# Two transformer layers on one core: x passed through DRAM, the scan's sum made by accumulating transfers, decay and state in shared buffers

## The chip, the cores and the metric

The kernel runs on one core of a Trainium2 chip. The time is device time in microseconds (us), the median of three runs. The five engines have queues of their own: PE (matrix products), DVE and POOL (elementwise work), ACT (activation functions), and SP, which here only issues transfers between DRAM and the on-chip memory. The on-chip memories are SBUF, and PSUM, in which PE's results arrive. One engine's instructions run in the order in which the program lists them; between engines, semaphores order them.

## What is computed

Eight batches of x, each 512 tokens by 256 features in float32, go through two layers with modulated layernorms. Shortened:

```python
# layer 0
h = layernorm(x) * (1 + ca) + sa
x = x + ga * gated_attention(h)            # q^T k over tokens, softmax, v * sum(attn) * gate
h = layernorm(x) * (1 + cb) + sb
x = x + gb * (shared_mlp(h) + top2_of_8_experts(h))
# layer 1, the mixer
h = layernorm(x) * (1 + ca) + sa
raw, gate = split(h @ W_in)
s  = silu(causal_conv(raw) + conv_b)       # 4 taps, 512 channels
ts, Bmat, C = split(s @ W_x)               # 64, 16 and 16 columns
dt = softplus(ts @ W_dt + b_dt)
for t in tokens:                           # state: 512 channels x 16
    state = exp(dt[t] * A) * state + dt[t] * Bmat[t] * s[t]
    y[t]  = sum_over_16(state * C[t])
x = x + ga * (((y + s * D) * silu(gate)) @ W_out)
# layer 1, the feed-forward: weights are -1, 0 or 1, with a scale per output
h = layernorm(x) * (1 + cb) + sb
x = x + gb * w3(gelu(h2(gelu(h1(silu(w1(h)) * w2(h))))))
```

ga and gb have at least 0.25 in magnitude. Each layer has its own sa, ca, ga, sb, cb, gb, one row per batch.

## The kernel before

**A plan.** No loop of the kernel issues instructions directly. The stages record operations with `op(engine, us, fn, r=, w=, need=, lead=, lat=)` (L100): a price in us, what is read and written, and a due time, which `run` (L1061) gives from the stage's start and the share of the stage that is done, less `lead`. `Plan.order` (L135) then simulates the five engines with these prices, takes on each free engine the ready operation that is due first (ACT adds LOOK to those that need another function table), and `emit` writes the instructions in the order of their planned starts. The order on each engine is thus fixed before the run; the times are not. An operation due later than the oldest unplaced one by more than AHEAD is held back (L203).

**Buffers.** A buffer that belongs to a pool (L249) takes a slot when its first operation is placed and gives it back after its last. The pools that matter here: `mm` with 5 PSUM banks for products, `v` with one, `st` with 2 slots of [128, 2, 512], `two` with 5, `xn` with 2, `big` with 8 (feed-forward activations), `hs`, `dt` and `y` with one each. x itself has three fixed slots (L1066); batch b uses slot b mod 3 from its load to the feed-forward.

**Stages.** For each batch (L1096 to L1104): `front` (the attention), `experts`, `mixer`, `ffn`, begun at b x TURN plus 0, FRONT, MIX_AT and FFN_AT. Since MIX_AT and FFN_AT come later than one and two turns, the front and experts of a batch stand beside the mixer of the one before and the ffn of the one before that. A first plan (L1073) holds the setup, the front of batch 0 and `test`, which rounds the 22 blocks of the feed-forward's weights (L1045) and compares them with the originals (L1046). If all are equal, the branch with split float32r activations runs, as it does with these inputs; the other branch is in the program and not run.

**The ends of layer 0.** The experts add their outputs in `acc` (L746, DVE), then POOL multiplies by gb (L751) and adds to x (L753).

**The mixer.** A layernorm of x into xn_m (L763), a transpose into hTm (L764), products ps_raw and the convolution into `hs`, ps_x, a small store of B and C to DRAM (`bc_d`), and dt by two halves of two channel chunks each, with `ab` and `lost` in `st` slots (L800). `y` begins as s times D (L828), hs becomes s times dt (L831). Then come 32 steps u, for 16 states d and two halves h (L844). The rows of B and C come back broadcast to all 128 partitions as brow and crow (L850), and ACT copies brow to PSUM as bp. ACT makes the decays, two exps of 511 columns, in one of three fixed buffers whose column 0 of each chunk is zero (L841). DVE multiplies v = hs x bp (L858) and scans the two chunks as one row of 1024 columns into `st` (L861); the zero restarts the second chunk. POOL multiplies st by crow (L864) and adds it to its half of y (L866). After the last step the gate products ps_g (L873), the product with y, and pa_m (L881); `add_gated` (L476) multiplies pa_m by ga on DVE and adds it to x on POOL.

**The ffn.** A layernorm of x into xn_g (L897), and x stored in `x_d` in DRAM (L898), from where it returns in two loads as `xo` at the end (L1012), is added to the transposed output and stored. Its activations (a_h_sh and a_h_sl are the high and low parts) go to float32r products, ps_h_s and pa_f (L988, L1002). All matrix products are recorded with line L343.

**Loads.** `load` (L313) records a DMA on SP with a lead of 12 us and a latency of 2.0; SP's queue is one list for weights, rows, x and stores. Weights are loaded anew for every batch.

Of the kernel before, what the change touches and what calls it, by code (L numbers as in the profile page):

```python
# [10 lines left out]
ALU = mybir.AluOpType  # L11
# [34 lines left out]
TURN, FRONT, EXPERTS = 235.0, 64.0, 124.5  # L46
MIX_AT, MIX = 221.7, 270.0
FFN_AT, FFN = 531.0, 249.5
FROM, UNTIL = 0.12, 0.949
LOOK = 16.226  # L50
DECAYS, BURST = 3, 1
EARLY, RUSH, SLOW, AHEAD = 19.951, 14.0, 4.404, 69.662
# [14 lines left out]
class Op:  # L67
    __slots__ = ("eng", "us", "fn", "due", "bufs", "succ", "npred", "avail", "lock", "table",
                 "start", "end", "lat", "n", "placed")


class Plan:
# [27 lines left out]
    def op(self, eng, us, fn, r=(), w=(), need=(), lock=False, table=None, lead=0.0, lat=0.0):  # L100
        o = Op()
        o.eng, o.us, o.fn, o.due, o.lock, o.table, o.lat = eng, us, fn, self.due - lead, lock, table, lat
        o.n, o.succ, o.npred, o.avail, o.placed = len(self.ops), [], 0, 0.0, False
# [31 lines left out]
    def order(self):  # L135
# [9 lines left out]
        t, left = 0.0, len(self.ops)  # L145

        def placeable(o):
            want, lines = {}, {}
            for b in o.bufs:
                if b.pool and b.slot is None:  # L150
                    want[b.pool] = want.get(b.pool, 0) + 1
                    if self.pools[b.pool][1]:
                        lines.setdefault(b.line, []).append(b)
# [6 lines left out]
        def place(o):  # L160
# [14 lines left out]
            if e == "SP":  # L175
                free[e] = t + 0.06
                dma = max(dma, t) + us
                o.end = dma + o.lat
            else:
                free[e] = o.end  # L180
                o.end += o.lat
# [10 lines left out]
            for s in o.succ:  # L192
                s.npred -= 1
                s.avail = max(s.avail, o.end + (0.0 if s.eng == e and e != "SP" else self.HOP))
# [4 lines left out]
        while left:  # L199
            placed = False  # L200
            while first < len(by_due) and by_due[first].placed:
                first += 1
            limit = by_due[first].due + self.ahead if first < len(by_due) else 0.0  # L203
# [25 lines left out]
            assert later, "nothing can be placed"  # L229
            t = min(later)  # L230
# [13 lines left out]
def block_kernel(ctx: ExitStack, tc: tile.TileContext, t: dict, out: bass.AP):  # L244
# [8 lines left out]
        "dt": (1, True), "y": (1, True), "sp": (1, True), "st": (2, True), "bcb": (1, True),  # L253
# [42 lines left out]

    for i in range(DECAYS):
        G.memset(fixed([P, 2, S], f"decay{i}").t, 0.0)

    def record(part):  # L300
# [5 lines left out]
        decay = [fixed([P, 2, S], f"decay{i}") for i in range(DECAYS)]  # L306
# [6 lines left out]
        def load(dst, kb, fn, r=(), part=None, lead=12.0, need=()):  # L313
            op("SP", kb * 0.0052, fn, r=r, w=[(dst, part)] if part is not None else [dst], lead=lead,
# [264 lines left out]
        def front(b, x):  # L579
# [76 lines left out]
            for m in range(CH):  # L656
# [5 lines left out]
                    pg.t, [(whgv()[:, k, ms], nT.t[:, k, :]) for k in range(KD)]), r=[whg, nT])  # L662
# [25 lines left out]
        def experts(b, x):  # L688
# [9 lines left out]
            for m in range(CH):  # L698
# [5 lines left out]
                    pv.t, [(w3v()[:, k, ms], hT.t[:, k, :]) for k in range(KD)]), r=[w3, hT])  # L704
# [48 lines left out]
            op("POOL", 2.4, lambda: G.tensor_tensor(x.t, x.t, acc.t, ALU.add), r=[acc], w=[x], lead=RUSH)  # L753


        def mixer(b, x):
# [6 lines left out]
            layernorm(x, xn, f"m{b}", RUSH)  # L763
# [72 lines left out]
            def exps(u):  # L836
                for v in range(u, u + BURST):
                    d, h = v // 2, v % 2
                    for i in range(2):
                        c = 2 * h + i  # L840
                        A.activation(decay[v % len(decay)].t[:, i, 1:], dt.t[:, c, 1:], AF.Exp,  # L841
                                     scale=neg_a.t[:, c, d : d + 1])

            for u in range(2 * DST):  # L844
                d, h = u // 2, u % 2
                da, cs = decay[u % len(decay)], slice(2 * h, 2 * h + 2)
# [7 lines left out]
                if u % BURST == 0:  # L854
                    op("ACT", 1.42 * BURST, lambda u=u: exps(u), r=[dt, neg_a],
                       w=[decay[v % len(decay)] for v in range(u, u + BURST)], table="exp", lead=SLOW)
# [3 lines left out]
                st = buf("st", [P, 2, S], f"st_{b}_{d}_{h}")  # L860
                op("DVE", 2.28, lambda v=v, st=st, da=da: V.tensor_tensor_scan(  # L861
                    st.t.rearrange("p c t -> p (c t)"), da.t.rearrange("p c t -> p (c t)"),
                    v.t.rearrange("p c t -> p (c t)"), 0.0, ALU.mult, ALU.add), r=[da, v], w=[st])
                op("POOL", 2.4, lambda st=st, cc=cc: G.tensor_tensor(  # L864
                    st.t, st.t, over_tokens(cc.t, 2), ALU.mult), r=[cc], w=[st])
                op("POOL", 2.4, lambda st=st, cs=cs: G.tensor_tensor(  # L866
                    y.t[:, cs, :], y.t[:, cs, :], st.t, ALU.add), r=[st], w=[(y, pair(h))])
# [12 lines left out]
            for j in range(NT // 2):  # L880
# [3 lines left out]
                add_gated(x, j, ps, ga, lambda: ga.t, f"tmpm_{b}_{j}")  # L884


        def ffn(b, x):
# [4 lines left out]
            half = 0.5 if fast else 1.0  # L892
# [4 lines left out]
            layernorm(x, xn, f"g{b}", RUSH)  # L897
            op("SP", 2.7, lambda: SP.dma_start(out=x_d[b].t, in_=x.t), r=[x], w=[x_d[b]], lat=2.0)  # L898
# [49 lines left out]
            for g in range(CF // 2):  # L948
                gs = slice(2 * g * P, (2 * g + 2) * P)
                w, (w1, w2) = weights(f"w_f{b}_{g}", [f1[:, :, gs], f2[:, :, gs]], g)  # L950
                for i in range(2):
# [6 lines left out]
                        pv.t, by(lambda k: w2()[:, k, ms], hT, KD)), r=[w] + every, share=half)  # L958
# [50 lines left out]
            for j in range(NT // 2):  # L1009
                ps, xo = mm(f"ps_o{b}_{j}"), buf("two", [P, 2, D], f"xo_{b}_{j}", line="xo")  # L1010
                js = slice(2 * j, 2 * j + 2)
                load(xo, 256, lambda xo=xo, js=js: SP.dma_start(out=xo.t, in_=x_d[b].t[:, js, :]), r=[x_d[b]], lead=RUSH)  # L1012
# [53 lines left out]
        slots_x = [fixed([P, NT, D], f"x_{i}") for i in range(3)]  # L1066
        xs = [slots_x[b % 3] for b in range(B)]
# [28 lines left out]
        for b in range(B):  # L1096
# [6 lines left out]
            run(mixer(b, xs[b]), b * TURN + MIX_AT, MIX)  # L1103
# [65 lines left out]
```

## Time and profile before

| | |
|---|---|
| median of 3 runs | 2246.09 us (2244.88 to 2247.49) |
| the profiled execution | 2246.68 us, its span 2244.9 us |
| mean granted clock of PE | 0.94 |
| moved over the span | 294.52 MB, mean 131 GB/s |

The profile is one execution. Where the stages of some batches stood, first to last start, in us from the start of the span:

| batch | qk | last product of experts (end) | ps_raw, first | first v to last v | pa_m | ps_o |
|---|---|---|---|---|---|---|
| 0 | 58.2 | 206.8 | 220.6 | 279.8 to 442.3 | 475.0 to 483.8 | 760.3 |
| 1 | 237.8 | 403.2 | 434.9 | 502.2 to 672.5 | 716.8 to 723.9 | 1013.7 |
| 2 | 461.4 | 654.0 | 678.0 | 743.2 to 913.0 | 959.0 to 972.9 | 1257.5 |
| 5 | 1206.3 | 1392.9 | 1413.9 | 1479.0 to 1655.5 | 1688.3 to 1702.3 | 1948.2 |
| 7 | 1691.8 | 1878.4 | 1899.5 | 1954.5 to 2102.8 | 2119.3 to 2126.4 | 2236.0 |

In rows of the profile, a group is a line, an engine and an operation with what it writes and reads; busy time and mean of one stand before the second bar's idle time, which is that of the engine just before such instructions, with what released it. A transfer's row has its size and the median from issue to landing.

### The profile page before, as it was taken

Reading aid. Unit: us, or ns where it says so; the run is one execution under the profiler, and the core shown is the slowest. Engines: PE = TensorE matmul, PEld = TensorE weight load, DVE = VectorE, ACT = ScalarE, POOL = GpSimd, SP = SyncE. Lnnn points to the kernel's source line nnn. Section 1 sums busy time; section 2 is a strip of 40 time slices with the busy share of each in tenths; the row PEclk is TensorE's granted clock in tenths of the full one; section 3 lists DMA queues with packets and bytes.
Section 4 is the critical chain, followed back from the end, with each engine's and each line's share of the span. In section 5 each row is a group of like instructions: output and inputs, shape, how many; then the busy total and the mean of one; then the engine's idle time right before and its main releaser. Section 6 shows DMA issues by size and latency. Waiting matters only on the chain.

```text
span 2244.9 us, 22011 instructions
## 1 busy us (share of the span) xinstructions
PE 1973.9 (88%) x6916; PEld 1292.8 (58%) x6916; DVE 1635.1 (73%) x2074; ACT 1691.8 (75%) x2433; POOL 1535.7 (68%) x765
## 2 busy tenths in 40 slices
PE   1897879498999899999999999999999999768587
PEld 0455336245775567656765577656765677445465
DVE  4532589869885898669895998679876988598531
ACT  3522768569987898788988898789988898779442
POOL 1201488969896788567895789678876789399700
PEclk6998889699999999999999999999999999979888
DMA  9226335223453345334443345334533443335333
GB/s 264 77 93 191 88 108 167 79 91 122 142 175 106 112 133 171 112 111 139 158 157 117 115 150 174 116 118 140 170 121 117 140 150 116 120 108 169 103 104 105
DMA packets 186608, 294.52 MB, mean 131 GB/s; under 512 B 14232, under 2 KB 109728, under 8 KB 186480
## 3 DMA queue, kind: packets, MB, share of 16 engines
q1 hardware_dynamic: 186480, 293.01, 41.3%
q8 instruction: 57, 0.93, 0.2%
q14 instruction: 71, 0.58, 0.1%
HBM read 283.94 MB, written 20.55 MB: 136 GB/s over the span
## 4 chain that ended last, share of the span: by engine, by line
PE 67%; POOL 10%; ACT 9%; DVE 9%; issue 3%; DMA 1%; SPq 0%; DVEq 0%; POOLq 0%; ACTq 0%
PE ps_h_s L343 17%; PE pa_e L343 9%; PE ps_e L343 9%; PE ps_sim L343 4%; POOL st L864 4%; POOL y L866 4%; PE pg L343 4%; DVE st L861 3%; PE pv L343 3%; PE pa_m L343 3%; PE ps_qk L343 2%; PE pa_f L343 2%; PE ps_g L343 2%; PE pa_o L343 2%; PE pa_s L343 2%
## 5 line engine op out<-in xcount | busy, mean ns | idle before, releaser
L864 POOL TENSOR_TENSOR st<-st,crow 128x1024 f32<-128x1024 f32 x256 | 608.5, 2377 | 167.4 <-DVE st L861 103.0
L866 POOL TENSOR_TENSOR y<-y,st 128x1024 f32<-128x1024 f32 x256 | 607.7, 2374 | 18.1
L861 DVE TENSOR_TENSOR_SCAN st<-decay,v 128x1024 f32<-128x1024 f32 x256 | 584.6, 2284 | 35.7 <-POOL y L866 17.4
L841 ACT ACTIVATE decay<-dt,neg_a 128x511 f32<-128x511 f32 x512 | 335.8, 713 | 46.5 <-DVE st L861 41.3
L858 DVE TENSOR_TENSOR v<-hs,bp 128x1024 f32<-128x1024 f32 x256 | 313.3, 1224 | 13.6 <-ACT bp L853 8.6
L343 PE MATMUL ps_h_s<-a_h_sh,w_f_h 128*128 128x512 f32 x512 | 212.0, 414 | 35.3 <-DVE a_h_sl L915 31.7
L343 PE MATMUL ps_h_s<-a1h,w_f_h 128*128 128x512 f32 x512 | 220.5, 431 | 16.0 <-DVE a1l L973 14.7
L343 PE MATMUL pa_e<-w_e,ge 128*128 128x256 f32 x1024 | 232.1, 379 | 1.4 <-ACT ge L735 1.4
L343 PE MATMUL ps_e<-hT,w_e 128*128 128x512 f32 x512 | 231.4, 592 | 0.0
L343 PEld LDWEIGHTS pa_e<-w_e,ge 128*128 128x128 f32 x1024 | 194.4, 190 | 44.6 <-issue 15.3
L343 PE MATMUL ps_h_s<-a_h_sl,w_f_h 128*128 128x512 f32 x512 | 204.8, 400 | 0.0
L343 PE MATMUL ps_h_s<-a1l,w_f_h 128*128 128x512 f32 x512 | 202.8, 396 | 0.0
L841 ACT ACT_TABLE_LOAD x146 | 187.3, 1283 | 4.0 <-DVE st L861 1.3
L746 DVE SCALAR_TENSOR_TENSOR acc<-pa_e,rt,acc 128x256 f32<-128x256 f32 x256 | 112.0, 477 | 87.3 <-PE pa_e L343 86.3
L991 ACT ACTIVATE a_h_sh<-ps_h_s,cols 128x512 fp32r<-128x512 f32 x128 | 88.0, 688 | 110.4 <-PE ps_h_s L343 109.4
L915 DVE TENSOR_TENSOR a_h_sl<-ps_h_s,a_h_sh 128x512 fp32r<-128x512 f32 x128 | 87.4, 683 | 96.1 <-ACT ps_h_s L991 95.6
L343 PEld LDWEIGHTS ps_e<-hT,w_e 128*128 128x128 f32 x512 | 97.2, 190 | 92.4 <-issue 79.4
L343 PEld LDWEIGHTS ps_h_s<-a_h_sh,w_f_h 128*128 128x128 f32 x512 | 99.0, 193 | 70.4 <-DVE a_h_sl L915 35.7
L343 PEld LDWEIGHTS ps_h_s<-a1h,w_f_h 128*128 128x128 f32 x512 | 97.9, 191 | 48.9 <-DVE a1l L973 15.5
L735 ACT ACTIVATE ge<-ps_e 128x512 f32<-128x512 f32 x128 | 73.8, 598 | 54.1 <-PE ps_e L343 53.5
L343 PEld LDWEIGHTS ps_h_s<-a1l,w_f_h 128*128 128x128 f32 x512 | 97.9, 191 | 28.0 <-issue 8.7
L343 PE MATMUL ps_sim<-k,q 128*128 128x512 f32 x256 | 113.8, 603 | 0.0
(212 smaller groups left out, 3821.4 us busy)
## 6 DMA issues: line engine op xcount, KB each, us to landing
w_f_h<-fw_d SPq DMA_DIRECT2D x128, 512.0 KB, 3.5
w_e<-in_ew SPq DMA_DIRECT2D x128, 256.0 KB, 3.0
brow<-bc_d SPq DMA_DIRECT2D x128, 256.0 KB, 3.7
crow<-bc_d SPq DMA_DIRECT2D x128, 256.0 KB, 3.9
w_f<-fw_d SPq DMA_DIRECT2D x48, 512.0 KB, 4.0
w_s<-in_sw SPq DMA_DIRECT2D x24, 512.0 KB, 5.6
test<-in_f_h SPq DMA_DIRECT2D x16, 512.0 KB, 7.3
fw_d<-in_f_h SPq DMA_DIRECT2D x16, 512.0 KB, 6.4
```

The costliest lines, as they stand in the source:

```text
L343: T.matmul(ps, lhsT=lhsT, rhs=rhs, start=(i == 0), stop=(i == last))
L735: op("ACT", 0.63, lambda ps=ps, g=ge[m]: A.activation(g.t, ps.t, AF.Gelu), r=[ps], w=[ge[m]], table="gelu", lead=RUSH)
L746: op("DVE", 0.48, lambda ps=ps, n=n, i=i, e=e: V.scalar_tensor_tensor(acc.t[:, n, :], ps.t[:, i * D : (i + 1) * D], comb(n, e), acc.t[:, n ...
L841: A.activation(decay[v % len(decay)].t[:, i, 1:], dt.t[:, c, 1:], AF.Exp, scale=neg_a.t[:, c, d : d + 1])
L858: op("DVE", 1.22, lambda v=v, cs=cs, bp=bp: V.tensor_tensor(v.t, hs.t[:, cs, :], over_tokens(bp.t, 2), ALU.mult), r=[hs, bp], w=[v])
L861: op("DVE", 2.28, lambda v=v, st=st, da=da: V.tensor_tensor_scan(st.t.rearrange("p c t -> p (c t)"), da.t.rearrange("p c t -> p (c t)"), v ...
L864: op("POOL", 2.4, lambda st=st, cc=cc: G.tensor_tensor(st.t, st.t, over_tokens(cc.t, 2), ALU.mult), r=[cc], w=[st])
L866: op("POOL", 2.4, lambda st=st, cs=cs: G.tensor_tensor(y.t[:, cs, :], y.t[:, cs, :], st.t, ALU.add), r=[st], w=[(y, pair(h))])
L915: op("DVE", 0.69, lambda: V.tensor_tensor(lo.t[:, at, :], ps.t, hi.t[:, at, :].bitcast(F32), ALU.subtract), r=[ps, (hi, at)], w=[(lo, at)] ...
L991: put(ps, nxt, m, lambda o, ps=ps, m=m, s=s: A.activation(o, ps.t, AF.Gelu, scale=col(s)[:, m : m + 1]), 0.69, [cols], table="gelu")
```

## The change

It has four parts, and new planner times.

- **x passes through DRAM.** The experts end with acc x gb + x in `acc`, which is stored in `x_d`. The mixer loads it for its layernorm, which works in place in xn; its tail loads x again in two halves (`xm`), adds the gated output in `tmp` and stores the halves in `x_d`. The ffn loads that, normalizes in place, and loads xo as before, now only once fT[0] stands. x has two fixed slots instead of three. `add_gated` is no longer called by the mixer.
- **y is summed by transfers.** The add of POOL (before: L866) becomes a DMA that POOL issues and that adds st to y in SBUF. It is ordered behind the multiply of its step and behind the last accumulate on the same half of y.
- **Decay and state share buffers.** The pool `st` has six slots instead of two; the exps, now of 512 columns, are written in the step's own st slot, and two scans of 512 columns work in place there. The three decay buffers and their clearing go.
- **Orders and planner.** Some products also need the buffers that their followers write (`need=`). The planner learns `move`, a DMA issued from POOL; loads are priced at 0.0032 us a KB instead of 0.0052; if nothing can be placed, the limit of AHEAD is lifted once (`stuck`). Mixer and ffn have turns of their own (TURN_M, TURN_F).

```diff
-TURN, FRONT, EXPERTS = 235.0, 64.0, 124.5
-MIX_AT, MIX = 221.7, 270.0
-FFN_AT, FFN = 531.0, 249.5
-FROM, UNTIL = 0.12, 0.949
-LOOK = 16.226
-DECAYS, BURST = 3, 1
-EARLY, RUSH, SLOW, AHEAD = 19.951, 14.0, 4.404, 69.662
+TURN, FRONT, EXPERTS = 210.53, 82.297, 147.593
+TURN_M, MIX_AT, MIX = 212.288, 264.782, 239.578
+TURN_F, FFN_AT, FFN = 215.967, 519.656, 225.321
+FROM, UNTIL = 0.193, 0.955
+LOOK = 40.478
+EARLY, RUSH, SLOW, AHEAD = 37.621, 10.554, -11.873, 136.563
...
-        "dt": (1, True), "y": (1, True), "sp": (1, True), "st": (2, True), "bcb": (1, True),
+        "dt": (1, True), "y": (1, True), "sp": (1, True), "st": (6, True), "bcb": (1, True),
...
-    for i in range(DECAYS):
-        G.memset(fixed([P, 2, S], f"decay{i}").t, 0.0)
...
-            op("POOL", 2.4, lambda: G.tensor_tensor(x.t, x.t, acc.t, ALU.add), r=[acc], w=[x], lead=RUSH)
+            op("POOL", 2.4, lambda: G.tensor_tensor(acc.t, acc.t, x.t, ALU.add), r=[x], w=[acc], lead=RUSH)
+            op("SP", 1.7, lambda: SP.dma_start(out=x_d[b].t, in_=acc.t), r=[acc], w=[(x_d[b], (0, 1))], lat=2.0,
+               lead=RUSH)
...
-            layernorm(x, xn, f"m{b}", RUSH)
+            load(xn, 512, lambda: SP.dma_start(out=xn.t, in_=x_d[b].t), r=[(x_d[b], (0, 1))])
+            layernorm(xn, xn, f"m{b}", RUSH)
...
+            def exps(u, st):
+                d, h = u // 2, u % 2
+                for i in range(2):
+                    c = 2 * h + i
+                    A.activation(st.t[:, i, :], dt.t[:, c, :], AF.Exp, scale=neg_a.t[:, c, d : d + 1])
+
+            def scans(v, st):
+
+                for i in range(2):
+                    V.tensor_tensor_scan(st.t[:, i, :], st.t[:, i, :], v.t[:, i, :], 0.0, ALU.mult, ALU.add)
...
-                st = buf("st", [P, 2, S], f"st_{b}_{d}_{h}")
-                op("DVE", 2.28, lambda v=v, st=st, da=da: V.tensor_tensor_scan(
-                    st.t.rearrange("p c t -> p (c t)"), da.t.rearrange("p c t -> p (c t)"),
-                    v.t.rearrange("p c t -> p (c t)"), 0.0, ALU.mult, ALU.add), r=[da, v], w=[st])
+                op("DVE", 2.35, lambda v=v, st=st: scans(v, st), r=[v], w=[st])
...
-                op("POOL", 2.4, lambda st=st, cs=cs: G.tensor_tensor(
-                    y.t[:, cs, :], y.t[:, cs, :], st.t, ALU.add), r=[st], w=[(y, pair(h))])
+                op("POOL", 0.88, lambda st=st, cs=cs: G.dma_start(
+                    out=y.t[:, cs, :], in_=st.t, accum_op=ALU.add), r=[st], w=[(y, pair(h))], move=2.8, lat=3.0)
...
-                add_gated(x, j, ps, ga, lambda: ga.t, f"tmpm_{b}_{j}")
+                tmp, xo = buf("two", [P, 2, D], f"tmpm_{b}_{j}", line="tmp"), buf("two", [P, 2, D], f"xm_{b}_{j}", line="xm")
+                js = slice(2 * j, 2 * j + 2)
+                load(xo, 256, lambda xo=xo, js=js: SP.dma_start(out=xo.t, in_=x_d[b].t[:, js, :]),
+                     r=[(x_d[b], j), (y, 0)], lead=RUSH, need=[tmp])
+                op("DVE", 0.69, lambda ps=ps, tmp=tmp: V.tensor_tensor(
+                    tmp.t, ps.t.rearrange("p (i d) -> p i d", i=2), over_tokens(ga.t, 2), ALU.mult),
+                    r=[ps, ga], w=[tmp], lead=RUSH)
+                op("POOL", 1.3, lambda tmp=tmp, xo=xo: G.tensor_tensor(tmp.t, tmp.t, xo.t, ALU.add),
+                   r=[xo], w=[tmp], lead=RUSH)
+                op("SP", 1.4, lambda tmp=tmp, js=js: SP.dma_start(out=x_d[b].t[:, js, :], in_=tmp.t),
+                   r=[tmp], w=[(x_d[b], j)], lat=2.0)
...
-            layernorm(x, xn, f"g{b}", RUSH)
-            op("SP", 2.7, lambda: SP.dma_start(out=x_d[b].t, in_=x.t), r=[x], w=[x_d[b]], lat=2.0)
+            load(xn, 512, lambda: SP.dma_start(out=xn.t, in_=x_d[b].t), r=[(x_d[b], (0, 1))])
+            layernorm(xn, xn, f"g{b}", RUSH)
...
+                     r=[(x_d[b], j), fT[0]], lead=RUSH)
...
-        slots_x = [fixed([P, NT, D], f"x_{i}") for i in range(3)]
-        xs = [slots_x[b % 3] for b in range(B)]
+        slots_x = [fixed([P, NT, D], f"x_{i}") for i in range(2)]
+        xs = [slots_x[b % 2] for b in range(B)]
...
-            run(mixer(b, xs[b]), b * TURN + MIX_AT, MIX)
-            run(ffn(b, xs[b]), b * TURN + FFN_AT, FFN)
+            run(mixer(b), b * TURN_M + MIX_AT, MIX)
+            run(ffn(b), b * TURN_F + FFN_AT, FFN)
```

## The prediction

> **What bounds it now.** I read the busy shares and the slices first, then single stretches, then what ends the waits. Columns of the slices: one digit per 56 us.
>
> ```profile
> PE 1973.9 (88%) x6916; PEld 1292.8 (58%) x6916; DVE 1635.1 (73%) x2074; ACT 1691.8 (75%) x2433; POOL 1535.7 (68%) x765
> ...
> PE   1897879498999899999999999999999999768587
> ...
> POOL 1201488969896788567895789678876789399700
> PEclk6998889699999999999999999999999999979888
> ```
>
> PE is at 88%, and its low digits stand at both ends: slices 2 to 8 and the last six. POOL is high just there. Three stretches tell the regimes apart: the first scan (batch 0), one turn of the middle, the last scan (batch 7).
>
> ```profile
> core 0: us, PE busy (x) PEld busy (x) DVE busy (x) ACT busy (x) POOL busy (x), PEclk, DMA share, GB/s
> 281.00:456.00 175.00, 123.83 (x373) 72.92 (x372) 150.76 (x173) 118.81 (x175) 159.78 (x75) 0.83 0.38 114
> 1206.30:1449.00 242.70, 236.00 (x858) 157.38 (x857) 199.78 (x250) 212.21 (x305) 190.59 (x94) 0.99 0.43 137
> 1955.00:2106.00 151.00, 98.31 (x341) 72.18 (x342) 130.76 (x97) 122.84 (x166) 144.00 (x62) 0.81 0.38 126
> ```
>
> In the middle PE is busy 236.0 of 242.7 us at a clock of 0.99: the turn is PE's, and nothing that only frees DVE, ACT or POOL shortens it. In the first and last scan PE has 124 of 175 and 98 of 151 us, and POOL 160 and 144: there the scan on POOL sets the pace. The rows of one scan step say why; busy and mean come first, then idle time and releaser.
>
> ```profile
> L864 POOL TENSOR_TENSOR st<-st,crow 128x1024 f32<-128x1024 f32 x256 | 608.5, 2377 | 167.4 <-DVE st L861 103.0
> L866 POOL TENSOR_TENSOR y<-y,st 128x1024 f32<-128x1024 f32 x256 | 607.7, 2374 | 18.1
> L861 DVE TENSOR_TENSOR_SCAN st<-decay,v 128x1024 f32<-128x1024 f32 x256 | 584.6, 2284 | 35.7 <-POOL y L866 17.4
> L841 ACT ACTIVATE decay<-dt,neg_a 128x511 f32<-128x511 f32 x512 | 335.8, 713 | 46.5 <-DVE st L861 41.3
> L858 DVE TENSOR_TENSOR v<-hs,bp 128x1024 f32<-128x1024 f32 x256 | 313.3, 1224 | 13.6 <-ACT bp L853 8.6
> ```
>
> A step costs POOL 2.377 + 2.374 = 4.75 us, and 32 x 4.75 = 152, the length of the last scan; DVE needs 2.284 + 1.224 = 3.51.
>
> ```profile
> DVE st L861 <- POOL y L866: 17.4, 20, 2.4
> ...
> PE ps_hTm L462 <- ACT xn_m L451: 36.8, 2, 26.8
> ```
>
> So DVE waits for POOL to free one of two state slots, ACT's exps for DVE to free a decay buffer (41.3 idle), and PE stands once for 26.8 us (batch 1's mixer, behind batch 0's scan). To measure PE I price each matmul by the spacing of its kind's starts (0.43 us an f32 record of 512 columns, 0.216 of 256, 0.229 for f32r): 1897 us in all, 235.5 a batch. Span less work, 348, is lost: 49 before the first qk (58.2), 102 by batch 0's dt, 168 by batch 2's qk, 230 by the end of batch 7's experts (1878.4), the rest behind them. The edit removes no matmul; it can win only from these losses.
>
> **The change, part by part.** *The add on y* leaves POOL: 256 x 2.374 = 608 us go, 256 issues come. No trace here has such an issue. Bounds: 0.1 us[...], and 2.37 (it holds POOL as long as the add did, no gain). I take 0.9, nearer the first[...]: the step is 2.38 + 0.9 = 3.28, under DVE's. POOL sets the pace again only from 2.377 + issue > 4.6, an issue of 2.2. Each accumulate waits for its multiply and for the accumulate two steps back (same half of y). Queued behind it on POOL is the next multiply; for that wait the state slots, now six, so exp and scan run several steps ahead before they feel it.
>
> Its landing: the 512 KB rows of SP are nearest.
>
> ```profile
> w_f_h<-fw_d SPq DMA_DIRECT2D x128, 512.0 KB, 3.5
> ...
> x<-in_x SPq DMA_DIRECT2D x8, 512.0 KB, 6.0
> ...
> x_d<-x SPq DMA_DIRECT2D x8, 512.0 KB, 2.7
> xo<-x_d SPq DMA_DIRECT2D x16, 256.0 KB, 4.0
> ```
>
> I take 5 us between 2.7 and 10 (twice the 3.5-row, and queueing[...]). A landing decides when two steps (2 x 4.7 = 9.4 us) are shorter than it.
>
> ```profile
> q1 hardware_dynamic: 186480, 293.01, 41.3%
> ```
>
> 293 MB in 0.413 x 2244.9 us is 316 GB/s, 1.66 us of all engines per 512 KB; head slices at full share show the same rate (264 GB/s in the first, partly idle). 32 accumulates a turn cost 53 us at 1.66 and 106 at twice that, x's four extra 512 KB passes 6.6: a share of 0.43 becomes 0.70 to 0.92 of a 235 us turn. By the row there is room. [...]brow and crow (3.7 and 3.9 us now) and the weights stand beside it. At 1.66 that costs nothing, as loads are issued ahead; at 3.3 the share of 0.92 would delay them, some 5 to 10 us a turn, 30 to 60 in all. I take the lower, and keep the other as a rival.
>
> *Scan in place, six slots, no decay buffers.* 256 scans become 512 of half the length. The fixed part of a DVE instruction comes from two rows of one kind: 1024 columns 1224 ns (L858), 2048 columns 2292 (hs times dt, L831), so 2 x 1224 - 2292 = 156 ns; the pair costs 2440, and 256 x 0.156 = 40 us of DVE are added. [...] It weighs where DVE now leads: +5 a scan at the ends; in the middle DVE goes from 199.8 to about 205 a turn and hides behind PE. The waits for slots (DVE's 17.4, ACT's 41.3) go, and ab and lost of both dt halves no longer take turns on two slots: batch 7's dt takes 17.5 us, of which about 10 go.
>
> *x through DRAM.* Per batch a store after the experts, a load for the mixer's layernorm, two quarter-megabyte loads and stores in its tail, a load for the ffn. Under PE's work in the middle: nothing, as another batch's products stand beside it; uncovered, a store and a load, 2.7 + 3.5 to 6.0 = 6.2 to 8.7 us, at the end where batch 7's tail has only the ffn behind it. In SP's queue the store waits for two 2.4 us operations of POOL, with weight loads queued behind it that PE needs next; if POOL is later than planned they are late by as much, up to 5 us a turn. I take nothing, as they are issued ahead of their use (they land in 3.5). xo now also waits for fT: 4.0 us beside the last products, nothing.
>
> *New times of the planner* move the order. Summed along PE's order, batch 0's dt stands at 191 us of matmul work (155 before), since front 1 goes ahead of mixer 0; batch 1's raw at 318 (276), batch 7's at 1668 (1668), batch 7's ffn unchanged at 1815 to 1897. Between raw 1 and raw 7 stand 1350 us instead of 1392. DVE's work in the scans is 160 at batch 0 (148), 184 to 189 in the middle (172), 142 at batch 7 (136), as more other work is interleaved. In the setup the 22 rounding casts all come before the first layernorm's xn_b (14 did): DMA-bound, about +5, returned as the tests no longer interleave with front 0.
>
> **The sum, on the profiled span of 2244.9.**
> A, start to the last v of batch 0: 442.3 now. Then: experts 0 end at 216 (206.8 + 5, + 4), 46 of front 1, 18 of mixer chain and stalls make dt 280; 17 to the first v; 160/0.95 = 168 of scan: 465. +22.
> B, to raw 7 (now 1899.5): 1350 of work. At the middle's ratio 242.7/235.5 it takes 1391, plus about 18 for batch 1, where little is left to interleave: 1409, raw 7 at 1874. So A and B: -25.
> C, raw 7 to the first v: 55.0 now, -10.
> D, the last scan: 151.4 by POOL now; 142/0.96 = 148 by DVE. -3.
> E, from its last scan to the end: 139.0 now. The last landing takes 2.4 + 0.9 + 2.7 to 6.4 instead of 4.75, +1 to +5; x's pass +6 to +9. +12.
> Together -26: span 2219; the run stood 1.8 above its span, so 2220. That run (2246.7) is 0.6 above the median of 2246.1, too little to correct for. -1.2%.
>
> **Rivals.**
> (1) The stalls go almost entirely: with POOL at 3.3 a step and six slots, B's 18 vanish, both end scans run at DVE's 0.99 (162 and 143, -11), and half of x's pass is hidden (-6): 2220 - 35 = 2185. For it: POOL is the top releaser of DVE in the scans. Against: front 1 is moved ahead of mixer 0, which starts the first scan later.
> (2) No change: what A does early is lost again to stalls in B (raw 7 at 1899), and C, D and E cancel: 2245. For it: batches 2 and 3 took 250 a turn (qk 461.4 to 962.5) with as much to interleave. Against: POOL, which ended those waits, is relieved.
> (3) Slower, by the accumulates' chain: at a landing of L the step can't be under L/2. It decides from 9.4 us. At 11.5 the scan takes 184: +16 in A, +36 in D, the middle covered (first to last scan there is 192): 2220 + 52 = 2272. For it: the accumulates share engines at 0.7 to 0.9, and landings of 6.0 to 7.3 stand in the saturated head. Against: 3.5 in the middle.
> (4) Slower, by DVE: if it reaches only 0.90 in the middle, 184/0.90 = 204 of scan and 44 of chain from raw to v make a turn of 248, +6 over six turns: 2260.
> That the planner's order isn't followed is no rival: each engine's list is fixed.
>
> **Chances.** Forecast 0.40, own range 2200 to 2240; (1) 0.28; (2) 0.09; (3) 0.14; (4) 0.09. Under 0.2% (4.5 us) a measurement here shows no change. Faster 0.68, same 0.09, slower 0.23. The range, 2165 to 2268, cuts the far ends of (1) and (3).
>
> **What would show it.** POOL's busy time near 930 (issues aren't counted) and its row of multiplies unchanged at 2377; scan rows of 512 columns near 1220; accumulates landing in 3 to 6 us; a DMA share of 0.65 to 0.75 in the middle; first v near 297, raw 7 near 1874; dt 7 in 8 us. Wrong: accumulates over 9 us, a POOL issue over 2 us, idle DVE before scans released by POOL, or turns in the middle away from 242.

## The result, and the profile after

The changed kernel takes 2230.02 us (median of 6 runs, 2223.38 to 2234.86) against 2245.39 us before (6 runs, 2240.05 to 2247.49). The ratio is 0.9933, with a 95% interval of 0.9915 to 0.9952: 15 us, or 0.7%, were gained. The profiled execution took 2229.34 us, its span is 2227.5.

The busy shares of the whole span, and three rows of the 40 slices (a digit is now 55.7 us):

```profile
PE 1972.2 (89%) x6916; PEld 1295.9 (58%) x6916; DVE 1626.7 (73%) x2330; ACT 1690.7 (76%) x2433; POOL 1161.8 (52%) x762
...
PE   1899996779999999999999999999999997685787
...
POOL 1212168844684568635773468355762666566300
DMA  9235569847887699949985899659894999599623
```

The DMA row of the kernel before:

```profile
DMA  9226335223453345334443345334533443335333
```

PE's work is the same and its share only 89% instead of 88. POOL has fallen from 68% to 52. The DMA row, which had 3 to 5 in the middle, now shows mostly 7 to 9, with a dip to 4 to 6 in each turn: what POOL lost went to the DMA engines. At the head PE's digits in slices 4 to 9 were 7, 8, 7, 9, 4, 9 and are 9, 9, 9, 6, 7, 7; those of the tail are as low as before.

The same three stretches as before the change: batch 0's scan, one turn of the middle (first qk of batch 5 to first qk of batch 6), batch 7's scan from its first v to the end of its last scan.

```profile
core 0: us, PE busy (x) PEld busy (x) DVE busy (x) ACT busy (x) POOL busy (x), PEclk, DMA share, GB/s
297.00:453.00 156.00, 117.98 (x362) 69.60 (x361) 146.25 (x193) 119.14 (x176) 123.10 (x79) 0.89 0.89 219
1096.90:1344.30 247.40, 239.24 (x857) 159.40 (x856) 197.98 (x284) 212.67 (x306) 145.63 (x95) 0.98 0.80 211
1924.80:2077.80 153.00, 90.32 (x296) 65.06 (x296) 133.86 (x137) 123.64 (x167) 101.38 (x64) 0.82 0.89 219
```

The turn of the middle is 247.4 us, longer than the 242.7 before, with PE busy 239.2: the neighbours (856.8 to 1096.9 and 1344.3 to 1586.7) take 240.1 and 242.4. The first scan takes 156 us instead of 175. The last takes 153.0 instead of 151.4, although POOL is busy only 101 of them instead of 144. DMA has a share of 0.80 to 0.89.

The rows of a scan step, with the line numbers of the changed kernel:

```profile
L877 POOL TENSOR_TENSOR st<-st,crow 128x1024 f32<-128x1024 f32 x256 | 626.9, 2454 | 336.4 <-DVE st L859 288.6
L859 DVE TENSOR_TENSOR_SCAN st<-st,v 128x512 f32<-128x512 f32 x512 | 596.1, 1205 | 13.1 <-DVE v L874 0.4
L854 ACT ACTIVATE st<-dt,neg_a 128x512 f32<-128x512 f32 x512 | 336.6, 713 | 34.5 <-DMA y<-st 30.2
L874 DVE TENSOR_TENSOR v<-hs,bp 128x1024 f32<-128x1024 f32 x256 | 312.3, 1220 | 24.0 <-ACT bp L870 21.3
L879 POOL DMA_DIRECT2D y<-st x256 | 227.0, 892 | 94.1 <-POOL st L877 49.7
```

The add of 2.37 us has become an issue of 0.89. DVE's wait on POOL is gone. The scans' busy time is the one to look at: 512 of a mean of 1205 ns would be 617 us, but their union is 596.1, so a pair is 2.33 us long and not 2.41; the two overlap by 0.08 us.

The queues and the transfers:

```profile
q0 software_dynamic: 36864, 134.23, 32.1%
...
y<-st POOLq DMA_DIRECT2D x256, 512.0 KB, 7.0
w_f_h<-fw_d SPq DMA_DIRECT2D x128, 512.0 KB, 5.2
...
brow<-bc_d SPq DMA_DIRECT2D x128, 256.0 KB, 5.2
```

The 256 accumulates take 0.321 x 2227.5 / 256 = 2.79 us of all 16 engines each, against the 1.66 that the prediction took from the queue before, and they land in 7.0. The loads of weights land in 5.2 instead of 3.5, brow in 5.2 instead of 3.7.

The waits that name the new transfers (us in total, times, longest):

```profile
POOL y L879 <- DMA y<-st: 35.6, 24, 3.1
...
ACT st L854 <- DMA y<-st: 30.2, 18, 6.6
```

POOL waits 35.6 us for an earlier accumulate on the same half of y. ACT waits 30.2 for a state slot, and 9.9 more with the load of a function table that stands before the exps. No other wait names the accumulates.

Where the span went, by the sections of the prediction (each last v is taken at its end):

| section | before | forecast | after |
|---|---|---|---|
| A, start to the last v of batch 0 | 442.3 | 465 | 450.6 |
| B, from there to raw of batch 7 | 1457.2 | 1409 | 1423.8 |
| C, to the first v of batch 7 | 55.0 | 45 | 50.4 |
| D, to the end of its last scan | 151.4 | 148 | 153.0 |
| E, to the end | 139.0 | 151 | 149.7 |
| span | 2244.9 | 2219 (2218 in these parts) | 2227.5 |

Raw of batch 7 stands at 1874.4, where 1874 was forecast, but by two errors that cancel: A is 14 us shorter than forecast and B 15 longer. C, D and E together are 9 longer.

### The profile page after: what moved, and what is told of

The parts are those of the page before. It is cut to its first block, busy times and chain, and to the rows that moved or that the text cites. A ratio compares the mean times of both kernels' runs of the same rounds, so it can differ in the third digit from the quotient of the medians.

```text
span 2227.5 us, 22743 instructions
## 1 busy us (share of the span) xinstructions
PE 1972.2 (89%) x6916; PEld 1295.9 (58%) x6916; DVE 1626.7 (73%) x2330; ACT 1690.7 (76%) x2433; POOL 1161.8 (52%) x762
## 5 line engine op out<-in xcount | busy, mean ns | idle before, releaser
L877 POOL TENSOR_TENSOR st<-st,crow 128x1024 f32<-128x1024 f32 x256 | 626.9, 2454 | 336.4 <-DVE st L859 288.6
L859 DVE TENSOR_TENSOR_SCAN st<-st,v 128x512 f32<-128x512 f32 x512 | 596.1, 1205 | 13.1 <-DVE v L874 0.4
L854 ACT ACTIVATE st<-dt,neg_a 128x512 f32<-128x512 f32 x512 | 336.6, 713 | 34.5 <-DMA y<-st 30.2
L879 POOL DMA_DIRECT2D y<-st x256 | 227.0, 892 | 94.1 <-POOL st L877 49.7
L353 PE MATMUL ps_h_s<-a_h_sh,w_f_h 128*128 128x512 f32 x512 | 221.6, 433 | 47.2 <-DVE a_h_sl L938 44.4
L353 PE MATMUL ps_h_s<-a_h_sl,w_f_h 128*128 128x512 f32 x512 | 209.4, 409 | 0.0
L829 POOL TENSOR_TENSOR lost<-ab,lost 128x1024 f32<-128x1024 f32 x16 | 37.7, 2354 | 154.1 <-DVE lost L827 154.1
L353 PEld LDWEIGHTS ps_h_s<-a_h_sl,w_f_h 128*128 128x128 f32 x512 | 102.0, 199 | 26.6 <-issue 5.5
```

What stands on the lines that cost most here:

```text
L353: T.matmul(ps, lhsT=lhsT, rhs=rhs, start=(i == 0), stop=(i == last))
L829: op("POOL", 2.4, lambda ab=ab, lost=lost: G.tensor_tensor(lost.t, ab.t, lost.t, ALU.subtract), r=[ab], w=[lost], lead=RUSH)
L854: A.activation(st.t[:, i, :], dt.t[:, c, :], AF.Exp, scale=neg_a.t[:, c, d : d + 1])
L859: V.tensor_tensor_scan(st.t[:, i, :], st.t[:, i, :], v.t[:, i, :], 0.0, ALU.mult, ALU.add)
L877: op("POOL", 2.4, lambda st=st, cc=cc: G.tensor_tensor(st.t, st.t, over_tokens(cc.t, 2), ALU.mult), r=[cc], w=[st])
L879: op("POOL", 0.88, lambda st=st, cs=cs: G.dma_start(out=y.t[:, cs, :], in_=st.t, accum_op=ALU.add), r=[st], w=[(y, pair(h))], move=2.8, la ...
```

## The experiments

My theory at first (A): the add, taken off POOL, is what pays. Rivals: the order that the new times plan is what pays (B), and the load of the accumulates on the DMA engines takes part of the gain away (C). Later: what the sixth slot and x's pass through DRAM are for. Each kernel is compared with the kernel before on its own chip; a difference between two kernels is that of their ratios times 2246 us. "Order kept" means that every engine has the list of the kernel named.

| kernel | median, us | ratio to before (95%) |
|---|---|---|
| changed | 2230.02 | 0.9933 (0.9915 to 0.9952) |
| after_pool_add | 2256.34 | 1.0038 (1.0024 to 1.0052) |
| after_plain_copy | 2217.68 | 0.9877 (0.9860 to 0.9895) |
| before_accum | 2479.52 | 1.1051 (1.1031 to 1.1071) |
| after_old_times | 2356.55 | 1.0488 (1.0468 to 1.0509) |
| before_slots | 2245.88 | 0.9993 (0.9986 to 1.0001) |
| before_slots_accum | 2268.54 | 1.0093 (1.0074 to 1.0112) |
| after_mix | 2220.95 | 0.9876 (0.9858 to 0.9894) |
| after_tail | 2219.96 | 0.9879 (0.9861 to 0.9896) |
| after_x_sbuf | 2257.47 | 1.0051 (1.0035 to 1.0068) |
| after_mix_half | 2215.92 | 0.9866 (0.9852 to 0.9880) |
| after_best | 2216.93 | 0.9865 (0.9849 to 0.9880) |
| after_five | 2247.06 | 0.9999 (0.9986 to 1.0012) |

### The add back on POOL, in the new order

```diff
-                op("POOL", 0.88, lambda st=st, cs=cs: G.dma_start(
-                    out=y.t[:, cs, :], in_=st.t, accum_op=ALU.add), r=[st], w=[(y, pair(h))], move=2.8, lat=3.0)
+                op("POOL", 0.88, lambda st=st, cs=cs: G.tensor_tensor(
+                    y.t[:, cs, :], y.t[:, cs, :], st.t, ALU.add), r=[st], w=[(y, pair(h))], move=2.8, lat=3.0)
```

The planner's prices are kept, so that every engine's order is that of the changed kernel.

> The changed kernel with the order of every engine kept, but y is added by POOL again (2.37 us) instead of by an accumulating transfer; six state slots, x through DRAM and the new times stay. Theory A (taking the add off POOL is what pays): the first and last scans are POOL's again at 2.45 + 2.37 = 4.8 us a step, 154 us against 156 and 152 now, and POOL goes to about 185 of 242 a turn in the middle, so its other work (adds on x, layernorms, lost) comes later: 2240 to 2255. Theory B (slots and new order pay, the add was only moved): 2225 to 2235. Theory C (the accumulates' load on the DMA engines takes away part of the gain): 2205 to 2220, with landings of w_f_h back at 3.5 us and middle turns at 240 or less.

It is 24 us slower than the changed kernel and even slower than the kernel before. So in the new order the accumulates are worth 24 us, and B is refuted as the sole cause. That order was planned with the accumulate's price; what a plan made for the add would reach with the new structure was not tried. Batch 0's scan and a turn of the middle, columns as in the windows above:

```profile
297.00:464.00 167.00, 123.83 (x364) 72.03 (x363) 146.60 (x194) 119.66 (x176) 161.38 (x78) 0.86 0.38 117
1119.80:1366.80 247.00, 239.09 (x858) 158.96 (x857) 198.91 (x284) 212.81 (x306) 192.31 (x95) 0.98 0.47 145
```

The scan of batch 0 is POOL's again: 161 of 167 us. The turns from batch 4 on are 245 to 249 us, against 240 to 247. There POOL, at 192 of 247 us, is late with its other work: ACT's wait for POOL's part of the mixer's layernorm is 31.2 us in all, where the changed kernel has 1.3. The last scan takes 152.9 us, as in the changed kernel.

```profile
ACT xn_m L461 <- POOL ln_m L458: 31.2, 7, 6.3
```

### The accumulate without the add

The transfer overwrites y; the sum over the states is left out.

```diff
-                    out=y.t[:, cs, :], in_=st.t, accum_op=ALU.add), r=[st], w=[(y, pair(h))], move=2.8, lat=3.0)
+                    out=y.t[:, cs, :], in_=st.t), r=[st], w=[(y, pair(h))], move=2.8, lat=3.0)
```

> The changed kernel, same order and same waits, but the transfer from st to y copies instead of adding (the sum over the states is left out). It measures what the accumulate costs more than a plain transfer of 512 KB, which is 1.66 us of the 16 engines at the rate of the other queue against 2.8 measured for the accumulate. Theory C: share of the engines in the middle from 0.8 to about 0.65, landings of weights from 5.2 to below 4.5 us, and 8 to 15 us less in all (2215 to 2222). Theories A and B: the load has cover, 2226 to 2232.

Queue and landings; the turn from batch 5's qk to batch 6's and the last scan; and the issue on POOL:

```profile
q0 software_dynamic: 36864, 134.23, 15.7%
...
y<-st POOLq DMA_DIRECT2D x256, 512.0 KB, 4.8
w_f_h<-fw_d SPq DMA_DIRECT2D x128, 512.0 KB, 4.2
```

```profile
1092.90:1336.10 243.20, 237.87 (x858) 158.12 (x858) 198.26 (x284) 212.53 (x306) 135.98 (x95) 0.99 0.66 217
1913.20:2065.90 152.70, 90.54 (x296) 65.52 (x296) 133.85 (x137) 123.58 (x167) 92.55 (x64) 0.79 0.65 220
```

```profile
L879 POOL DMA_DIRECT2D y<-st x256 | 152.2, 595 | 60.7 <-POOL st L877 52.0 <-DMA y<-st 5.0 <-issue 3.3
```

The same bytes cost 0.157 x 2215.8 / 256 = 1.36 us of the engines instead of 2.79, land in 4.8 instead of 7.0, and are issued in 0.60 us instead of 0.89. DMA's share in the middle falls from 0.80 to 0.66, weights land in 4.2, and the time falls by 13 us. C is shown: adding in the transfer instead of copying took 13 us of the gain. That POOL is also held 0.3 us less a step is not the cause: with half of the adds on POOL (below) it is busier and the time is as low. By which wait the adding costs is not told apart. Several are shorter with the copy: ACT's for state slots (13 us instead of 40), POOL's for y (5 instead of 36), and those of PE that name a transfer (22 us in all instead of 32). The place is seen in the sections: B is 1414.6 instead of 1423.8 (raw of batch 7 at 1862.8 less the last v of batch 0 at 448.2), while the last scan takes 152.7, as in the changed kernel. So the adding costs mostly in the middle, and the last scan does not wait for it.

### The accumulate alone, and the slots alone, in the old order

First only the add was exchanged in the kernel before, order kept, two state slots:

> The kernel before with its order kept, its two state slots and x in SBUF, but y summed by accumulating transfers from POOL's queue. Theory A taken alone (only POOL's 4.75 us a step bound the scans): the first and last scans fall to DVE's 3.5 to 4.4 a step, 2220 to 2235. With slots as the condition (mine): a state slot is now held for scan 2.3 + multiply 2.4 + issue 0.9 + landing 4 to 7 = 9.6 to 12.6 us, so with two slots a step takes 4.8 to 6.3 us instead of 4.75: first and last scan 154 to 202, middle covered up to 192: 2245 to 2330, most likely 2270.

```profile
DVE st L861 <- DMA y<-st: 302.9, 141, 7.8
```

This is DVE's wait for a state slot: 302.9 us in 141 waits, where the kernel before had 17.4 for POOL. A slot is now held until the transfer has landed (6.3 us), and the step takes up to 6.8 us (batch 3: 218.4 us for 32 steps; batch 0: 211.3). The mechanism was as expected, the size (2270, at most 2330) was not: I had held a scan of up to 192 us for covered in the middle, but the scans took 202 to 218 there and the turns went to 270 us.

Then the slots alone, in the same order, x in SBUF, five shared buffers:

```diff
+    free_st = list(range(5))
...
-                        A.activation(decay[v % len(decay)].t[:, i, 1:], dt.t[:, c, 1:], AF.Exp,
-                                     scale=neg_a.t[:, c, d : d + 1])
+                    A.activation(st.t[:, i, :], dt.t[:, c, :], AF.Exp, scale=neg_a.t[:, c, d : d + 1])
...
-                    st.t.rearrange("p c t -> p (c t)"), da.t.rearrange("p c t -> p (c t)"),
-                    v.t.rearrange("p c t -> p (c t)"), 0.0, ALU.mult, ALU.add), r=[da, v], w=[st])
+                    V.tensor_tensor_scan(st.t[:, i, :], st.t[:, i, :], v.t[:, i, :], 0.0, ALU.mult, ALU.add)
```

The planner still counts two slots and three decays; the buffers are taken, when the instructions are written, from five free ones.

> The kernel before, with the order of every engine kept and x in SBUF, but decay and state in five shared buffers: exps of 512 columns into the step's own buffer, two scans of 512 columns in place; POOL still adds. The split alone: a pair of scans is spaced 2.33 us in the changed kernel's trace against 2.284 for one of 1024, 0.05 x 256 = 12 us of DVE, which at the ends only POOL's pace can hide. Theory 'slots pay by themselves': DVE's 17 us and ACT's 41 us of waits for buffers go and the time falls to 2225 to 2238. Mine: POOL keeps 4.75 us a step and the order is the same, so nothing comes of it: 2240 to 2250.

> The same with y summed by accumulating transfers. Theory A (slots and accumulate together are the gain): the first scan falls from 175 to about 155 us and the last from 151 to about 142, DVE's pace, and batch 1's wait shrinks: 2215 to 2235. Theory B (the order planned with the new times is what pays, the order of before was planned around POOL's 4.75 us a step): 2240 to 2262. If five slots are still too few for landings of 6 us, the scan waits for y's transfers, and it is slower than before_slots.

A turn of the middle and the last scan (columns as before) of before_slots, and then of before_slots_accum:

```profile
1206.10:1448.80 242.70, 236.14 (x858) 157.25 (x857) 200.76 (x282) 211.13 (x303) 190.68 (x94) 0.99 0.44 137
1955.30:2103.20 147.90, 98.68 (x337) 72.18 (x338) 132.52 (x129) 123.24 (x167) 140.65 (x60) 0.79 0.41 128
```

```profile
1211.90:1459.10 247.20, 238.23 (x858) 158.18 (x857) 199.68 (x282) 212.43 (x305) 143.89 (x95) 0.99 0.77 203
1972.80:2131.20 158.40, 100.53 (x338) 73.66 (x339) 132.76 (x130) 123.84 (x167) 100.59 (x62) 0.79 0.90 221
```

The slots and the split scan alone change nothing (0.9993). With the accumulates on top it is 22 us slower: POOL is relieved by 47 and 40 us, PE, DVE and ACT have the same work, and yet both stretches are longer, the last scan by 10 us. The waits that name transfers have grown:

```profile
ACT st L855 <- DMA y<-st: 39.2, 22, 3.9
ACT bp L870 <- DMA brow<-bc_d: 18.3, 14, 3.0
PE ps_h_s L356 <- DMA w_f_h<-fw_d: 16.8, 16, 3.3
```

Without the accumulates the first is not there, the second is 1.0 us and the third 3.8. So rows and weights come late beside the accumulates; in the last scan PE's wait for weights alone is 10.2 us instead of 2.8. ACT also waits for slots that a transfer still reads, but DVE's idle time before the scans is only 14.0 us in all. How the 22 us divide between the late loads and the held slots is not shown.

Together these four runs are a square, and my theory A falls with it:

| | POOL adds | transfers add |
|---|---|---|
| order of before, x in SBUF, five slots | 0.9993 | 1.0093 |
| order of after, x through DRAM, six slots | 1.0038 | 0.9933 |

Each half alone makes the kernel slower, by 0.4 and 0.9% of the time before; both together are 0.7% faster. The square keeps two orders as they are, and each was planned for one way of adding; a plan of the structure before with the new times was not run.

### The times of before with the new structure

All six lines of constants as before (TURN_M and TURN_F 235.0), the order planned anew.

> The changed kernel with the planner's constants of before (one turn of 235.0, mixer at 221.7, ffn at 531.0, LOOK 16.2, AHEAD 69.7 and so on); everything else stays, the order is planned anew. Theory A: the parts pay by themselves, 2222 to 2238. Theory B (the order is what pays): 2245 to 2270.

It is 125 us slower than the changed kernel, where B had allowed 15 to 40. One turn of the middle:

```profile
992.20:1253.80 261.60, 243.19 (x857) 161.68 (x856) 200.88 (x283) 215.87 (x307) 145.70 (x94) 0.95 0.76 200
```

PE is busy 243.2 of 261.6 us: 18 us a turn are small waits for many things, none above 10 us in two turns. That the times fit the structure is thus worth more than any one part of it that was taken back with the new times (24, 26 and 15 us in the sections on the add, on x and on the sixth slot); which of the constants it is was not tried.

### Part of the adds on POOL

POOL is busy 52% in the changed kernel, and DMA 80%. So some adds were given back, the order kept:

```diff
-                op("POOL", 0.88, lambda st=st, cs=cs: G.dma_start(
-                    out=y.t[:, cs, :], in_=st.t, accum_op=ALU.add), r=[st], w=[(y, pair(h))], move=2.8, lat=3.0)
+                op("POOL", 0.88, (lambda st=st, cs=cs: G.tensor_tensor(
+                    y.t[:, cs, :], y.t[:, cs, :], st.t, ALU.add)) if u % 4 == 1 else (lambda st=st, cs=cs: G.dma_start(
+                    out=y.t[:, cs, :], in_=st.t, accum_op=ALU.add)), r=[st], w=[(y, pair(h))], move=2.8, lat=3.0)
```

> The changed kernel, order kept, with every fourth add (u % 4 == 1) on POOL and the others by transfer. All adds on POOL cost 26 us, the accumulates' weight on the DMA engines about 12 us. If the costs are linear: a quarter of 26 less a quarter of 12 and more is 2228 to 2234. If POOL has room for a quarter (52% busy, 3.7 us a step against DVE's 4.7) and only the last three quarters hurt: 2220 to 2227.

> As after_mix, with every second add on POOL (all of one half of y). After_mix gained 9 of the 12 us that the plain copy had shown to be had. If the DMA load is what remains: 2216 to 2221. If POOL's load returns (4.05 us a step on average, 4.8 in the steps that add): 2222 to 2240.

With a quarter on POOL the time falls by 13 us, with half (u % 2 == 1) by 15. A turn of the middle and the last scan with half:

```profile
1095.90:1337.70 241.80, 236.34 (x858) 157.35 (x857) 197.78 (x284) 212.49 (x306) 168.45 (x95) 0.99 0.64 182
1917.00:2066.60 149.60, 89.18 (x296) 64.64 (x296) 133.77 (x136) 122.75 (x166) 121.91 (x63) 0.81 0.66 171
```

DMA's share is 0.64 and 0.66, as with the plain copy, and POOL is busy 168 of 242 us. The 13 us that the adding cost are won back, and POOL isn't the bound. The costs are not linear: all adds on POOL cost 24 us, while half of them there, with half of the accumulates gone from the DMA engines, gain 15.

### The end of the last batch

after_tail keeps batch 7's x in SBUF (no store, no loads of x, `add_gated` on it) and puts its last two adds on POOL; the order after that is planned anew. after_best adds the quarter of the adds on POOL. For batch 7 alone:

```diff
+            if b == B - 1:
+                op("POOL", 2.4, lambda: G.tensor_tensor(x.t, x.t, acc.t, ALU.add), r=[acc], w=[x], lead=RUSH)
+                return
...
-            layernorm(xn, xn, f"m{b}", RUSH)
+            layernorm(xn if b < B - 1 else x, xn, f"m{b}", RUSH)
...
+                if b == B - 1:
+                    add_gated(x, j, ps, ga, lambda: ga.t, f"tmpm_{b}_{j}")
+                    continue
```

> The changed kernel with the last batch's x kept in its SBUF slot to the end (no store and no loads of x for it), and its last two adds on POOL. If the tail of batch 7 is the chain I took it for: pa_m to hTf falls from 14 to about 5.5 us and the last multiply to pa_m from 13 to about 9, 10 to 13 us less: 2217 to 2221. If PE's other work fills these gaps anyway: 2226 to 2232.

> After_mix and after_tail together. If the two act in different places (the middle and the end), their gains of 9 and 10 us add up: 2208 to 2214. If both are gains on the last scan and its tail: 2215 to 2221.

after_tail gained 12 us by the medians, and 5.7 between the two profiled executions, only partly where I had expected it. From the end of pa_m (2103.8) to hTf (2112.5) it is 8.7 us instead of 14.1, so x's pass costs 5.4 there (the kernel before takes 5.4 us for this stretch); from the last multiply to pa_m it is longer, 19.4 instead of 15.5. The stretch from the last scan to the end went from 149.7 to 146.8 only; the last scan itself went from 153.0 to 144.4 in the new order of that stretch, while raw of batch 7 came 5.8 later. What DVE waits for in the last scan, in the changed kernel (1924.8 to 2077.8) and then in after_tail (1930.6 to 2075.0):

```profile
DVE v L874 <- ACT bp L870: 11.6, 8, 2.4
```

```profile
DVE v L878 <- ACT bp L874: 1.5, 1, 1.5
```

v needs bp, the copy of brow that ACT makes. So the new order has nearly removed this wait, and that covers what the last scan gained.

The gains don't add up: after_best is level with after_mix_half. Both beat the two kernels, by 15 us the changed one and by 30 the one before.

### x in SBUF, and five slots

after_x_sbuf takes back the change's first part for every batch, which needs the third slot of x; after_five has x through DRAM. Both have five state slots:

```diff
-        "dt": (1, True), "y": (1, True), "sp": (1, True), "st": (6, True), "bcb": (1, True),
+        "dt": (1, True), "y": (1, True), "sp": (1, True), "st": (5, True), "bcb": (1, True),
```

> The changed kernel with x kept in SBUF as before (three slots, added in place, stored once for xo), which leaves five state slots instead of six; accumulates, in-place scans and the new times stay, the order is planned anew. If the pass through DRAM is only a cost (2 MB more a batch, and 8.7 us in the last batch's tail): 2215 to 2224. If the sixth slot and x's early release are needed for the new order: 2236 to 2260. If the new times fit only the very structure they were made for: over 2260.

> The changed kernel with five state slots instead of six, x through DRAM as in the change, the order planned anew. It parts the two things that after_x_sbuf changed at once (27 us slower). If the sixth slot is what the 27 us pay for: 2245 to 2262. If it is x's way (early release of its buffer, no additions to x on POOL behind products): 2226 to 2236.

after_x_sbuf is 26 us slower than the changed kernel, and after_five, in which only the pool `st` is five instead of six, is 15 slower. So about 15 go with the sixth slot, and about 12 with x's way. In after_x_sbuf POOL waits long for the mixer's products before it can add them to x, which the changed kernel's trace has in another form (47.0 us for tmpm):

```profile
POOL x L490 <- DVE tmpm L487: 70.6, 11, 26.2
```

DVE's layernorm for the ffn then waits 14.9 us for these adds on POOL.

Both were planned anew, and after_old_times shows what an order can do by itself; how much of the 15 and 12 us is the slot or x, and how much an order that its times don't fit, stays open. That x's pass is not merely a cost is shown for these times only.

## Why the prediction was right or wrong

The time is in the range and in the forecast's own range; 15 us of the 26 came. That A was forecast 14 us too long and B 15 too short is luck: it put raw of batch 7 where it is. By its steps:

**What bounds it.** Right: PE sets the turns of the middle (busy 239.2 of 247.4 us in batch 5's), and POOL's 4.75 us a step the first scan, as the returned add shows (161 of 167 us). For the last scan it was wrong. Without POOL's pace it takes 153.0 us and not 148; in before_slots, with POOL's adds, 147.9. Adding in the transfer is not the cause in the new order, since the plain copy has 152.7. The forecast gave DVE 0.96 of this stretch; it is busy 134 of 153 us, and 11.6 of the 19 idle ones it waits for bp (12.0 with the plain copy, 11.4 with the add on POOL, 1.1 before the change). The order on ACT, which copies brow to bp among the ffn's activations, is the term that was left out. No run changed that order alone.

**The add on y.** The issue was right to 1% (0.9; measured 0.892), but 0.9 was a choice between two bounds and not derived, so this is luck; the lower bound of 0.1 was too low: SP's issues in the trace before take at least 0.29 us, 0.37 in the median. The landing, 5, is 7.0. The multiply's row, forecast unchanged at 2377, is 2454. The mis-sized term is the weight on the engines: I took the 1.66 us per 512 KB of the loads "by the row" and kept "twice that" as a rival, with a share of 0.70 or 0.92. Measured are 2.79 us and a share of 0.80 to 0.83 in the turns of the middle; and this costs 13 us, which the plain copy and the mixes show. I had put the rival's cost at 30 to 60 us for 0.92. Of the 15 us that B was short, the profile of the plain copy accounts for 9; the rest is open. Beside POOL's transfers the most frequent loads of SP's queue land 1.5 to 1.8 us later than before: w_f_h in 5.2 instead of 3.5, w_e in 4.7 instead of 3.0, brow in 5.2 instead of 3.7, crow in 5.7 instead of 3.9.

**Scan in place.** The forecast took 156 ns of fixed part for each of 256 added scans, 40 us of DVE. Measured are 596.1 - 584.6 = 11.5 us, 0.045 a pair. Two things were wrong. The rows from which the 156 came are not of one kind: v reads bp in PSUM, hs times dt reads SBUF alone; what that makes of the 156 was not measured. And I added durations: 2 x 1.205 is 0.126 more than 2.284, but the second scan starts 0.08 us before the first has ended. The overlap is also why A came out shorter than forecast. The durations of DVE's instructions from the first v of batch 0 to the end of its last scan add up to 158.8 us, near the 160 forecast; but most neighbours overlap as the two scans do, and DVE is busy for only 147.7 us of the 157.5. In before_slots, where the scans take 595.9 us in all, even these 11 us cost nothing (0.9993).

**The slots.** I had six slots as a help for the wait on the accumulates. They are its condition: with two, in the old order, the time is 10.5% longer. The products of dt of batch 7 take 9.4 us and not 17.5, as forecast within 2; C fell by 4.6 and not by 10.

**x through DRAM.** E was right: 149.7 against 151. From pa_m to hTf batch 7 takes 14.1 us instead of 5.4, so the pass costs 8.7, where 6 to 9 was forecast. That it costs nothing in the middle was not measured by itself: with these times x in SBUF was slower, a gain that I hadn't looked for.

**New times of the planner.** I read them as a moved order with a few us in each section. They are a condition of the gain: without them the new structure is 5% slower than before. The forecast didn't need that, as it was made on the order itself; as an account of why the kernel is faster it was one-sided.

**Rivals.** (1), the stalls gone, did not come: half of the adds on POOL, the fastest measured here, takes 2216 where it had 2185. (2), no change, missed by 15 us. (3), the accumulates' chain, isn't reached: landings of 7.0 are under the 9.4 us from which it decides, POOL's wait for it is 35.6 us in all. (4), a DVE at 0.90, fails: the scans of the middle take 184 to 189 us from first v to last scan and not 204. Its sum was also off: 6 us over six turns on 2220 is 2256 and not 2260.

## What to carry to other kernels

Here a transfer that adds cost the DMA engines about twice a copy (2.79 us of all 16 per 512 KB against 1.36). Before moving an engine's work to them, sum their share per turn, and stop where both resources have slack: here a quarter or half of the adds left on POOL gained alike, 13 and 15 us. A state slot was held here until its transfer had landed (6.3 us in before_accum, where the scans waited 302.9 us for slots), so slots must come with such a transfer. And when a planned order and a structure are changed together, test the square of both: here each alone was slower, and neither explains the gain.

## What was not expected of the hardware

The accumulate from SBUF to SBUF took 2.79 us of the 16 engines per 512 KB against 1.36 for the same transfer without the add, and POOL needed 892 ns to issue it against 595. Two scans of 512 columns in a row took 2.33 us together although each shows 1.205; 1518 of the 2330 DVE instructions of the changed kernel start before the one in front has ended, by a median of 0.08 us.
